# Dealing the C products of a selective scan to two engines by a fixed list, with turned pairs alternating

## The chip, the core and the metric

The kernel runs on one core of a Trainium2 chip. The core has five engines with instruction queues of their own, each worked off in order: TensorE (PE, its weight loads shown as PEld), VectorE (DVE), ScalarE (ACT), GpSimd (POOL) and SyncE (SP), which issues the transfers. The metric is the device time in microseconds (us) of one execution. The profile is one execution recorded by the hardware profiler; its span runs from the first to the last instruction of the core.

## The reference

Four images of 64 x 64 positions and 192 channels pass through four layers, called a, b, c and d in the kernel. Each layer normalizes the image, projects it, applies a short depthwise convolution and SiLU, runs a selective state-space scan along one or four orders of the positions, gates the result, projects it back and adds it to the image. The scan of one order is what matters here:

```python
xz = xs @ in_w.T ; u, z = split(xz)
uc = silu(conv(u) + cb)
dt, B, C = split(uc @ xw.T, [12, 28])        # 12 + 16 + 16 values per position
delta = softplus(dt @ dtw.T + dtb)
def step(h, inp):                            # along the positions
    dA = exp(delta[:, None] * A)             # A: channels x 16 states
    h = dA * h + (delta * u)[:, None] * B[None, :]
    y = (h * C[None, :]).sum(states)
    return h, y
```

Layers a, b and d have 384 channels in the scan, layer c has 192. Layer b scans one order of the positions, the others four. Layer a's recurrence starts anew at every row or column of 64 positions, the others run through all 4096.

## The kernel before

Everything is float32. The channels lie on the partitions, in `nb` blocks of `P`: 3 blocks of 128 for layers a, b and d, and 2 blocks of 96 for layer c. The positions are cut into chunks of `T` = 512. The 16 states of a chunk are taken in 8 pairs `j` of `NT` = 2. The unit of work is a tile: one chunk, one pair and one block, 512 positions of two states side by side, so a row of 1024 values on each partition. A chunk has 24 tiles for `nb` = 3 and 16 for `nb` = 2, in the order pair by pair, and within a pair block by block. There are 13 orders of 8 chunks in an image, 104 chunks, and 416 in the whole run: 128 each in a, c and d, 32 in b.

A tile needs these pieces of work:

- `decay`: two exponentials on ACT give dA (L534).
- `inflow` (L540): on POOL, u = du * B, where du = delta * x is the chunk's and B was spread over the partitions by a transfer. A pair whose index is in `TURNED` does it otherwise: ACT scales the transposed du by B (`scaled`, L546, 8 operations for a pair), and PE transposes the products back into PSUM (`turned_inflow`, L555, 8 transposes for a tile).
- `scan` (L564): on DVE, the recurrence h = dA * h + u; one instruction of 1024 in layer a, two of 512 in the others.
- `save_carry` (L584): the last state is kept for the next chunk; on ACT if POOL multiplies by C, else on DVE. Layer a has none.
- `outflow` (L592): the product h * C, on POOL where `pool_c` is true, else on DVE.
- `total` (L599): 8 PE transposes add the product into `py` in PSUM, and `store` (L620) copies it out by ACT and sends it off.

The buffers matter. Each tile takes one of two PSUM buffers `ps`: an ordinary tile holds dA there and reads u from SBUF, a turned tile holds u there and reads dA from SBUF. If POOL multiplies by C, the scan writes h to one of four SBUF buffers, and the PSUM buffer is free after the scan; otherwise h goes to PSUM, which is free only after the product. There are three u buffers, three for POOL's products (`cp`), two for DVE's (`c`), and four for the scaled du (`dut`).

The order on each engine is written out by hand: `keep` (L273) ties each instruction to the one before it on its engine. The loop at L661 goes over steps s, one for each tile, and issues in step s: decay of tile s+1 (of s+2 if turned), turned inflow of s+1, the scaled operations due, scan of s, ordinary inflow of s+3, POOL's product of s-1, DVE's product of s, store of s-3, and PE's totals of s-1 (DVE's product) or s-3 (POOL's). At the end of the step follows a piece of the preparation of the next chunk, by the table `at` (L472 and L479): x_proj (`p_px`), its copy and transfer (`p_dbl`), dt_proj (`p_pd`), bias (`p_pre`), `p_softplus` with its change of the activation table, `p_du` (L428), and the transposes of du.

Which engine takes a product is decided at L499 to L513 by a running count: a share of 5 in 8 goes to POOL in layer a, 2 in 3 in the others. The count runs on from chunk to chunk, so that the pattern differs between chunks, and the last pair of a chunk always goes to DVE.

Of the kernel before, what the change touches and what calls it, by code (L numbers as in the profile page):

```python
# [7 lines left out]
F32 = mybir.dt.float32  # L8
AF = mybir.ActivationFunctionType
ALU = mybir.AluOpType  # L10
# [11 lines left out]
NS = 16  # L22
DR = 12
NT = 2
TB = T // 128

TURNED = {3: (2, 4, 6, 7), 2: (1, 3, 5, 7)}
CONV_ROWS = 16
CONV_SPLIT = 37
POOL_SHORT = 5, 8  # L30
POOL_LONG = 2, 3
GN_EPS = 1e-5
LN_EPS = 1e-5

# [11 lines left out]
class Net:  # L46
# [226 lines left out]
    def keep(self, ins):  # L273

        engine = ins.ins.engine
        prev = self.pinned.get(engine)
        if prev is not None:
            self.tc.add_manual_dep(
                ins.ins, prev.name,
                mybir.DependencyInfo(mybir.DependencyClass.NoSync, mybir.DependencyReason.DATA),  # L280
                reason="program order",
            )
        self.pinned[engine] = ins.ins
        return ins

    def scans(self, sp, pp, dp, xc, P, nb, dirs, short):
# [14 lines left out]
        nc, keep = self.nc, self.keep  # L301
        zeros = None
        if short:
# [5 lines left out]
            for rev in sorted({job[2] for job in dirs}):  # L309
                fixed[rev] = []  # L310
                for k in range(3):
                    f = sp.tile([P, NT, T], F32, tag=f"dAs{rev}{k}", bufs=1, name=f"dAs{rev}{k}_a")
# [50 lines left out]
        for i in range(len(dirs)):  # L363
            for ci in range(NCH)[:: -1 if dirs[i][2] else 1]:
                c = Chunk()
# [15 lines left out]
        def channels(c, b):  # L381
            return view(xc, b, c.ci, c.o.cols) if c.xs is None else rows(c.xs[:, b, :])
# [10 lines left out]
        def spare(c, shape, name):  # L393
            return bank(max(c.n - 1, 0), nb, shape, name)

        def p_px(b):
            def f(c):
                if b == 0:
                    c.px = spare(c, [DR + 2 * NS, T], f"px_{c.key}")
                keep(nc.tensor.matmul(  # L400
                    c.px, c.o.xw[:, b, :], channels(c, b), start=b == 0, stop=b == nb - 1
                ))
            return f
# [8 lines left out]
        def p_pd(b):  # L412
            def f(c):
                c.pd = spare(c, [P, T], f"pd_{c.key}{b}")
                keep(nc.tensor.matmul(
                    c.pd, c.o.dtw[:, b * P : (b + 1) * P], c.dbl[:DR, :], start=True, stop=True
                ))
            return f

        def p_pre(b):  # L420
            def f(c):
                keep(nc.scalar.activation(c.delta[:, b, :], c.pd, AF.Identity, bias=c.o.vec[:, b, 0:1]))
            return f
# [4 lines left out]
        def p_du(c):  # L428
            c.du = sp.tile([P, nb, T], F32, tag="du", bufs=2, name=f"du_{c.key}")
            if c.xs is not None:  # L430
                x = c.xs.rearrange("p b (r w) -> p b r w", w=W)
            elif c.o.cols:
                x = xc.rearrange("p b (h w) -> p b h w", w=W)
                x = x[:, :, :, c.ci * R : (c.ci + 1) * R].rearrange("p b h w -> p b w h")
            else:
                x = xc.rearrange("p b (h w) -> p b h w", w=W)[:, :, c.ci * R : (c.ci + 1) * R, :]
            du, delta = (v.rearrange("p b (r w) -> p b r w", w=W) for v in (c.du, c.delta))
            keep(nc.gpsimd.tensor_tensor(du, delta, x, ALU.mult))

        def p_turn_B(c):  # L440
            c.tb = spare(c, [128, TB, DR + 2 * NS], f"tb_{c.key}")
# [11 lines left out]
        def p_turn_du(b):  # L453
            def f(c):
                c.td = spare(c, [128, TB, P], f"td_{c.key}{b}")
                for q in range(TB):
                    keep(nc.tensor.transpose(
                        c.td[:, q, :], c.du[:, b, q * 128 : (q + 1) * 128], self.ident[:P, :P]
                    ))
            return f  # L460
# [9 lines left out]

        if nb > 2:
            at = {  # L472
                0: [p_dir], 3: [p_px(0), p_px(1)], 4: [p_px(2)], 5: [p_dbl, p_const], 6: [p_pd(0)],
                7: [p_pre(0)], 8: [p_pd(1)], 9: [p_pre(1)], 10: [p_pd(2)], 11: [p_pre(2)],
                12: [p_softplus, p_turn_B], 13: [p_du, p_BT], 15: [p_turn_du(0)], 16: [p_duT(0)],
                17: [p_turn_du(1)], 18: [p_duT(1)], 19: [p_turn_du(2)], 20: [p_duT(2)],
            }
        else:
            at = {  # L479
                1: [p_dir], 3: [p_px(0), p_px(1)], 4: [p_dbl], 5: [p_const, p_pd(0)], 6: [p_pre(0)],  # L480
                7: [p_pd(1)], 8: [p_pre(1), p_softplus, p_turn_B], 9: [p_du, p_BT],
                10: [p_turn_du(0)], 11: [p_duT(0)], 12: [p_turn_du(1)], 13: [p_duT(1)],
            }
# [13 lines left out]
            pass  # L497

        per_chunk = NS // NT * nb  # L499
        share = POOL_SHORT if short else POOL_LONG  # L500
        tiles, due, turns = [], 0, 0
        for n, c in enumerate(chunks):
            c.n = n
            for j in range(NS // NT):
                for b in range(nb):
                    t = Tile()
                    t.c, t.b, t.j, t.n0 = c, b, j, j * NT
                    t.turned = j in TURNED[nb]
                    t.turn = turns
                    turns += t.turned  # L510
                    t.starts = b == 0
                    t.pool_c = j + 1 < NS // NT and due >= share[1]
                    due += share[0] - (share[1] if t.pool_c else 0)  # L513
                    t.key = f"{c.key}_{t.n0}{b}"
                    tiles.append(t)

# [29 lines left out]
        def scaled(c, n, q):  # L546
            if q == 0:
                c.scaled[n] = sp.tile(
                    [128, TB, nb * P], F32, tag="dut", bufs=4, name=f"dut_{c.key}_{n}"
                )  # L550
            keep(nc.scalar.activation(  # L551
                c.scaled[n][:, q, :], c.duT[:, q, :], AF.Copy, scale=c.BT[:, q, n : n + 1]
            ))
# [66 lines left out]
        def store(t):  # L620
            c, b, o = t.c, t.b, t.c.o
            if b == 0:
                c.yt = sp.tile([128, TB, nb * P], F32, tag="yt", bufs=1, name=f"yt_{c.key}")
            keep(nc.scalar.copy(c.yt[:, :, b * P : (b + 1) * P], c.py[b]))
            if b < nb - 1:
                return
            if not o.cols:
                keep(nc.sync.dma_start(
                    o.out[c.ci * T : (c.ci + 1) * T].rearrange("(q p) c -> p q c", p=128), c.yt
                ))  # L630
                return
            dst = o.out.rearrange("(h w) c -> h w c", w=W)[:, c.ci * R : (c.ci + 1) * R]
            dst = dst.rearrange("h (q k) c -> k h q c", k=128 // H)
            for k in range(128 // H):
                keep(nc.sync.dma_start(dst[k], c.yt[k * H : (k + 1) * H]))
# [10 lines left out]
        N = len(tiles)  # L646
# [11 lines left out]
                inflow(t)  # L658
        for op in scales.get(-1, []):
            scaled(*op)  # L660
        for s in range(N + 4):  # L661
            t = tiles[s] if s < N else None
            if s + 1 < N and not tiles[s + 1].turned:
                decay(tiles[s + 1])
            if s + 2 < N and tiles[s + 2].turned:
                decay(tiles[s + 2])
            if s + 1 < N and tiles[s + 1].turned:
                turned_inflow(tiles[s + 1])
            for op in scales.get(s, []):
                scaled(*op)  # L670
            if t:
                scan(t)
                if not t.pool_c and not short:
                    save_carry(t)
            if 2 <= s < N + 2 and tiles[s - 2].pool_c and not short:
                save_carry(tiles[s - 2])
            if s + 6 < N and tiles[s + 6].starts and not tiles[s + 6].turned:
                load_B(tiles[s + 6])
            if s + 3 < N and tiles[s + 3].starts:
                load_C(tiles[s + 3])  # L680
            if s + 3 < N and not tiles[s + 3].turned:
                inflow(tiles[s + 3])
            if 0 < s <= N and tiles[s - 1].pool_c:
                outflow(tiles[s - 1], nc.gpsimd)
            if t and not t.pool_c:
                outflow(t, nc.vector)
            if 3 <= s < N + 3 and tiles[s - 3].j == NS // NT - 1:
                store(tiles[s - 3])

            if 0 < s <= N and not tiles[s - 1].pool_c:  # L690
                total(tiles[s - 1])
            if 3 <= s < N + 3 and tiles[s - 3].pool_c:
                total(tiles[s - 3])
            if t and t.c.n + 1 < len(chunks):
                for f in at.get(s - t.c.n * per_chunk, []):
                    f(chunks[t.c.n + 1])
# [370 lines left out]
```

## Time and profile before

| What | us |
|---|---|
| median of 3 runs | 34516.05 (34504.28 to 34522.61) |
| profiled execution, device time | 34507.41 |
| its span | 34505.6 |
| DVE busy | 28332.2 (82%) |
| POOL busy | 25842.7 (75%) |
| PE busy | 24862.7 (72%) |
| ACT busy | 23542.8 (68%) |

The four images repeat one pattern of about 8620 us. In the first, the scans of layer a run from 302 to 2700 us of the span, those of b from 3250 to 3864, of c from 4117 to 5688, and of d from 5974 to 8437. A view of stretches gives each engine's busy time in each of these. The view of waits tells which instruction had an engine idle before it and what ended that idle time; "issue" there means that the profile shows nothing that ended it. In the timeline, equal instructions in a row are merged into one line with their count.

### The profile page before, as it was taken

The numbers are of one execution on the slowest core, as the hardware profiler recorded it, in microseconds if no ns is written. First come the engines' busy times: TensorE is split into PE (matmuls) and PEld (weight loads), VectorE is DVE, ScalarE is ACT, GpSimd is POOL, SyncE is SP. The second block draws the span as 40 slices with busy tenths as digits, with TensorE's granted clock in tenths as the row PEclk, the third lists the DMA queues.
The fourth block names the chain that finished last, engine by engine and source line by source line (L and its number), as shares of the span: only waits on it lengthen the run. The fifth ranks groups of instructions, "written<-read, shape, count | busy, mean of one in ns | idle before, by whom it ended". The sixth has DMA issues, their size and how long they took to land. (4 is left out here: it accounts for less than half of the span.)

```text
span 34505.6 us, 390569 instructions
## 1 busy us (share of the span) xinstructions
PE 24862.7 (72%) x135240; PEld 18214.6 (53%) x135240; DVE 28332.2 (82%) x23900; ACT 23542.8 (68%) x44285; POOL 25842.7 (75%) x11310
## 2 busy tenths in 40 slices
PE   7778777766777877776677787777667778777666
PEld 4554554554455455455445545545544554554554
DVE  8885798887888579888888857988878885798887
ACT  6773686776677368677667736867766773686776
POOL 5883696887688369688768836968876883696887
PEclk8888877888888877787888888778888888877888
DMA  3332333223333233322333322332233332233223
GB/s 111 107 106 79 92 106 100 93 94 115 109 105 108 78 91 106 101 93 94 115 109 106 107 79 92 107 100 93 94 115 109 105 108 78 91 106 101 93 96 111
DMA packets 1390794, 3455.73 MB, mean 100 GB/s; under 512 B 184736, under 2 KB 632080, under 8 KB 1382672
## 3 DMA queue, kind: packets, MB, share of 16 engines
q1 hardware_dynamic: 1388816, 3430.74, 31.3%
q8 instruction: 1073, 17.58, 0.2%
q14 instruction: 905, 7.41, 0.1%
HBM read 2975.18 MB, written 455.08 MB: 99 GB/s over the span
## 5 line engine op out<-in xcount | busy, mean ns | idle before, releaser
L615 PE MATMUL py_d<-ident,c_d 128*128 128x128 f32 x24576 | 3812.3, 314 | 2151.3 <-POOL c_d L597 1320.1
L615 PE MATMUL py_a<-ident,c_a 128*128 128x128 f32 x24576 | 3628.5, 302 | 2206.4 <-POOL c_a L597 1136.1
L597 POOL TENSOR_TENSOR c_d<-h_d,C_d 128x1024 f32<-128x1024 f32 x2036 | 4778.0, 2367 | 167.7 <-DVE h_d L580 164.9
L597 POOL TENSOR_TENSOR c_a<-h_a,C_a 128x1024 f32<-128x1024 f32 x1908 | 4478.4, 2370 | 422.9 <-issue 287.4
L615 PEld LDWEIGHTS py_d<-ident,c_d 128*128 128x128 f32 x24576 | 3356.9, 164 | 2603.5 <-POOL c_d L597 1640.3
L615 PEld LDWEIGHTS py_a<-ident,c_a 128*128 128x128 f32 x24576 | 3149.0, 156 | 2515.3 <-DVE c_a L597 1269.2
L542 POOL TENSOR_TENSOR u_d<-du_d,B_d 128x1024 f32<-128x1024 f32 x1536 | 3619.2, 2360 | 899.4 <-issue 885.6
L542 POOL TENSOR_TENSOR u_a<-du_a,B_a 128x1024 f32<-128x1024 f32 x1536 | 3606.6, 2363 | 715.9 <-DVE h_a L573 696.1
L597 POOL TENSOR_TENSOR c_c<-h_c,C_c 96x1024 f32<-96x1024 f32 x1356 | 3178.2, 2360 | 383.9 <-DVE h_c L580 361.1
L580 DVE TENSOR_TENSOR_SCAN h_d<-dA_d,carry_d,u_d 128x512 f32<-128x512 f32 x2536 | 3073.0, 1264 | 333.1 <-POOL c_d L597 263.6
L534 ACT ACTIVATE dA_d<-delta_d,A_d 128x512 f32<-128x512 f32 x3072 | 2118.1, 690 | 1638.0 <-DVE c_d L597 1492.5
L534 ACT ACTIVATE dA_a<-delta_a,A_a 128x512 f32<-128x512 f32 x3072 | 2119.7, 690 | 1248.8 <-DVE c_a L597 1087.6
L615 PE MATMUL py_c<-ident,c_c 96*128 96x96 f32 x16384 | 2237.3, 304 | 864.9 <-DVE c_c L597 671.9
L573 DVE TENSOR_TENSOR_SCAN h_a<-dA_a,u_a 128x1024 f32<-128x1024 f32 x1140 | 2579.5, 2281 | 328.2 <-ACT dA_a L538 175.2
L615 PEld LDWEIGHTS py_c<-ident,c_c 96*128 96x128 f32 x16384 | 2031.1, 181 | 1194.6 <-DVE c_c L597 794.4
L542 POOL TENSOR_TENSOR u_c<-du_c,B_c 96x1024 f32<-96x1024 f32 x1024 | 2411.2, 2361 | 6.3 <-DVE dA_c L580 6.0
L559 PE MATMUL ut_d<-ident,dut_d 128*128 128x128 f32 x12288 | 1913.5, 307 | 615.7 <-DVE c_d L597 589.7
L580 DVE TENSOR_TENSOR_SCAN ut_d<-dAs_d,carry_d,ut_d 128x512 f32<-128x512 f32 x1536 | 1970.8, 1283 | 395.7 <-issue 172.5
L551 ACT ACTIVATE dut_a<-duT_a,BT_a 128x384 f32<-128x384 f32 x4096 | 2291.1, 604 | 0.0
L551 ACT ACTIVATE dut_d<-duT_d,BT_d 128x384 f32<-128x384 f32 x4096 | 2290.6, 601 | 0.0
L534 ACT ACTIVATE dAs_d<-delta_d,A_d 128x512 f32<-128x512 f32 x3072 | 2042.7, 713 | 298.4 <-DVE h_d L580 230.6
L559 PEld LDWEIGHTS ut_d<-ident,dut_d 128*128 128x128 f32 x12288 | 1589.3, 159 | 1136.9 <-issue 921.3
(364 smaller groups left out, 63113.7 us busy)
## 6 DMA issues: line engine op xcount, KB each, us to landing
C_a<-bc_a SPq DMA_DIRECT2D x1024, 512.0 KB
C_d<-bc_d SPq DMA_DIRECT2D x1024, 512.0 KB
C_c<-bc_c SPq DMA_DIRECT2D x1024, 384.0 KB
B_a<-bc_a SPq DMA_DIRECT2D x512, 512.0 KB
B_d<-bc_d SPq DMA_DIRECT2D x512, 512.0 KB
B_c<-bc_c SPq DMA_DIRECT2D x512, 384.0 KB
C_b<-bc_b SPq DMA_DIRECT2D x256, 512.0 KB
xd_a<-xo_a SPq DMA_DIRECT2D x48, 2048.0 KB
```

What stands on the lines that cost most here:

```text
L534: keep(nc.scalar.activation(out, delta, AF.Exp, scale=o.A[:, t.b, k : k + 1]))
L542: keep(nc.gpsimd.tensor_tensor(t.u, t.c.du[:, t.b, None, :].to_broadcast([P, NT, T]), t.c.B[t.j], ALU.mult))
L551: keep(nc.scalar.activation(c.scaled[n][:, q, :], c.duT[:, q, :], AF.Copy, scale=c.BT[:, q, n : n + 1]))
L559: keep(nc.tensor.transpose(t.u[:, n, q * 128 : (q + 1) * 128], t.c.scaled[t.n0 + n][:, q, t.b * P : (t.b + 1) * P], self.ident,))
L573: keep(nc.vector.tensor_tensor_scan(hf, af, uf, 0.0, ALU.mult, ALU.add))
L580: keep(nc.vector.tensor_tensor_scan(hf, af, uf, o.carry[:, t.b, k : k + 1], ALU.mult, ALU.add))
L597: keep(engine.tensor_tensor(t.cm, t.h, t.c.C[t.j], ALU.mult))
L615: keep(nc.tensor.matmul(c.py[b][:, q, :], t.cm[:, n, q * 128 : (q + 1) * 128], self.ident[:P, :P], start=first, stop=c.sums[b] == NS and q ...
```

## The change

`TURNED` becomes 1, 3, 5, 7 for all layers; layers a, b and d had 2, 4, 6, 7, and layer c already had the new list. So ordinary and turned pairs alternate. The count of turned pairs stays four in eight.

The running count is replaced by a string for each number of blocks, one letter for each tile of a chunk, p for POOL and d for DVE, the same in every chunk: 17 p of 24, and 11 p of 16. The last pair is no longer kept for DVE.

In layers a, b and d the preparation is rearranged: x_proj's three matmuls stand in steps 3, 4 and 5 in place of 3, 3 and 4; the copy, the transfer of B and C, the constants of a new order and the first two blocks of dt_proj and bias come one step later; and du is computed on DVE in place of POOL, in the same step 13. Layer c keeps du on POOL and its table.

The buffers for scaled du go from four to three, and the store comes one step later, at s-4, so the loop runs one step longer.

```diff
-TURNED = {3: (2, 4, 6, 7), 2: (1, 3, 5, 7)}
+TURNED = 1, 3, 5, 7
-POOL_SHORT = 5, 8
-POOL_LONG = 2, 3
+PRODUCTS = {3: "dpdpppppdpppdpdpppdpdppp", 2: "ppdpdpppdpdpppdp"}
...
-            keep(nc.gpsimd.tensor_tensor(du, delta, x, ALU.mult))
+            keep((nc.vector if nb > 2 else nc.gpsimd).tensor_tensor(du, delta, x, ALU.mult))
...
-                0: [p_dir], 3: [p_px(0), p_px(1)], 4: [p_px(2)], 5: [p_dbl, p_const], 6: [p_pd(0)],
-                7: [p_pre(0)], 8: [p_pd(1)], 9: [p_pre(1)], 10: [p_pd(2)], 11: [p_pre(2)],
+                0: [p_dir], 3: [p_px(0)], 4: [p_px(1)], 5: [p_px(2)], 6: [p_dbl, p_const],
+                7: [p_pd(0)], 8: [p_pre(0)], 9: [p_pd(1)], 10: [p_pre(1), p_pd(2)], 11: [p_pre(2)],
                 12: [p_softplus, p_turn_B], 13: [p_du, p_BT], 15: [p_turn_du(0)], 16: [p_duT(0)],
...
-        share = POOL_SHORT if short else POOL_LONG
-        tiles, due, turns = [], 0, 0
+        tiles, turns = [], 0
...
-                    t.turned = j in TURNED[nb]
+                    t.turned = j in TURNED
...
-                    t.pool_c = j + 1 < NS // NT and due >= share[1]
-                    due += share[0] - (share[1] if t.pool_c else 0)
+                    t.pool_c = PRODUCTS[nb][len(tiles) % per_chunk] == "p"
...
-                    [128, TB, nb * P], F32, tag="dut", bufs=4, name=f"dut_{c.key}_{n}"
+                    [128, TB, nb * P], F32, tag="dut", bufs=3, name=f"dut_{c.key}_{n}"
...
-        for s in range(N + 4):
+        for s in range(N + 5):
...
-            if 3 <= s < N + 3 and tiles[s - 3].j == NS // NT - 1:
-                store(tiles[s - 3])
+            if 4 <= s < N + 4 and tiles[s - 4].j == NS // NT - 1:
+                store(tiles[s - 4])
```

## The prediction

> **What bounds the kernel now.** On the page I read the busy shares first: DVE 82%, POOL 75%, an average over stages. So I took the four scan stages of the first image apart, in the view of stretches (length, then PE, PEld, DVE, ACT and POOL busy):
>
> ```profile
> 302.00:2700.00 2398.00, 1705.79 (x10844) 1367.17 (x10844) 2076.25 (x1065) 1882.82 (x3384) 2104.30 (x893) 0.84 0.32 105
> 3250.00:3864.00 614.00, 433.53 (x2682) 363.16 (x2683) 548.50 (x514) 454.39 (x859) 528.92 (x225) 0.81 0.26 87
> 4117.00:5688.00 1571.00, 1165.24 (x6875) 926.60 (x6874) 1453.13 (x1366) 1262.82 (x2716) 1452.73 (x628) 0.71 0.34 105
> 5974.00:8437.00 2463.00, 1706.55 (x10268) 1364.95 (x10268) 2192.40 (x2051) 1854.90 (x3503) 2186.18 (x927) 0.81 0.28 92
> ```
>
> Over 32, 8, 32 and 32 chunks this is 74.9 us a chunk in a, 76.8 in b, 49.1 in c, 77.0 in d. In d DVE works 68.5 and POOL 68.3 of the 77.0: two engines nearly equal, both idle 8.5 us. Neither is the bound alone; they wait in turns. POOL's timeline in d shows where:
>
> ```profile
> 7119.29 4.67 POOL L542 TENSOR_TENSOR u_d<-du_d,B_d 128x1024 f32<-128x1024 f32 x2
> 7131.02 2.35 POOL L542 TENSOR_TENSOR u_d<-du_d,B_d 128x1024 f32<-128x1024 f32 x1 [7.06 <-issue]
> ...
> 7175.74 3.44 POOL L438 TENSOR_TENSOR du_d<-delta_d,xc_d 128x1536 f32<-128x1536 f32 x1
> 7179.13 2.36 POOL L542 TENSOR_TENSOR u_d<-du_d,B_d 128x1024 f32<-128x1024 f32 x1
> 7181.45 9.35 POOL L597 TENSOR_TENSOR c_d<-h_d,C_d 128x1024 f32<-128x1024 f32 x4
> ```
>
> The 7 us hole comes once a chunk (221 us, 32 times, in d's waits). It is the turned pairs 6 and 7 in a row: six tiles without an inflow, and the last three products held for DVE, so POOL runs dry, and its next inflow needs a u buffer that the scan of the next chunk's first tile frees. In the other 18 steps the same POOL is full (the lines after the hole run end to end), and there DVE waits for it, directly or through PE:
>
> ```profile
> DVE h_d L580 <- POOL c_d L597: 65.9, 32, 2.2
> DVE h_d L580 <- PE ut_d L559: 57.4, 33, 3.5
> DVE ut_d L580 <- issue: 45.7, 33, 2.9
> ```
>
> PE is in this list because a turned inflow stands behind totals that wait for POOL's products. In a it is the same: POOL waits 5.4 us a chunk for a u buffer (173.9 / 32) and DVE 5.7 for PE (182.6 / 32).
>
> [...]Every scan and product here has one input in PSUM; du on DVE has both in SBUF. [...]the one such instruction beside a busy POOL took 2642 ns against 559 on its own:
>
> ```profile
> L354 DVE TENSOR_TENSOR dgD_a<-ident,ds_a x4: 559/2642/2647, 272.7 to 2041.7; 128x384 f32<-128x384 f32 x4
> ```
>
> So the wait was 2.08 us, inside one POOL instruction. [...]
>
> **The change, part by part.** Durations are distances from start to start in the timelines: a POOL operation of 1024 takes 2.32 (9.35 / 4 less the overhang), a DVE tile with POOL's product 2.37 in d and 2.19 in a, one with DVE's own product and carry 3.90 in d and 3.45 in a.
>
> *Products.* Per chunk POOL's count is now 1908/128 = 14.9 in a, 15.6 in b, 10.6 in c, 15.9 in d; it becomes 17, 17, 11, 17. Over the run 504 products move: POOL +504 x 2.32 = +1169 us. DVE loses 1.26 for each in a (268) and about 1.53 elsewhere (236): -699.
>
> *du.* 288 leave POOL: 128 x 3.52 + 32 x 3.44 + 128 x 3.83 = -1051 us. No row shows it on DVE. [...]To this comes the wait for POOL's current instruction, 0 to 2.34, I take 1.0. POOL in turn stands for about 1.65. In half of d's chunks x is strided by 256 bytes, which cost POOL 4.2 in place of 3.4; on DVE 0 to 1.7 more there, I take 0.2 a chunk of d on the mean. Sum: DVE +288 x 2.7 = +780, POOL +475.
>
> So neither engine gets less work: POOL +590, DVE +80. What the change can bring is idle time alone, 8.5 us a chunk on each.
>
> *Turned pairs.* Every six tiles now have three inflows. I followed the queues by hand through one chunk. POOL's order is u6 u7 c3 u8 c4 c5 c6 c7 u12 u13 c9 u14 c10 c11 c13 u18 u19 c15 u20 c16 c17 c19 u0 u1 c21 u2 c22 c23 c1, 29 operations. In a, laid end to end from 0, c3 starts at 4.7, c9 at 23, c21 at 56, c1 at 65; DVE, held back only by u and by the four h buffers, ends those scans at least 4 us earlier each time. POOL never runs dry: 29 x 2.32 + 1.65 = **69.0** a chunk, DVE needing only 17 x 2.19 + 7 x 3.45 + 2.7 = 64.1. In d DVE needs 17 x 2.37 + 7 x 3.90 + 2.9 = **70.5**, POOL 69.0; the least slack of POOL behind a scan is about 3 us (c1). In c, POOL has 19 x 2.32 + 2.6 = **46.7**, DVE 11 x 2.36 + 5 x 3.86 = 45.3.
>
> *The preparation.* ACT must end the softplus (two table loads of 1.28 around 1.49) before du. Counting from the start of scan 12: decay 1.4, two scaled 1.1, load and softplus 2.8, so 5.3; DVE reaches du at 3.9 + 2.4 = 6.3. Then reload and decay of tile 14 end at about 8.0, while du ends at 8 to 9: du lies partly in a gap that tile 14 would leave anyway. Without that cover it costs its 2.7. PE's transposes of du, which waited 2.5 us on POOL's du (74.8 in 30 times in d), find it done. x_proj's split, and B's transfer one step later, are hidden: first use is 12 steps on. The later store and three dut buffers: the third buffer is wanted in the step after the transposes that free it; 0, at most 0.5 a chunk. SP's queue gains no transfer. *Drain:* the last three products of a stage now end on POOL: +2.5 in each of 16 stages, +40.
>
> I add idle time for in-order stalls: 1.3 in a, 1.5 in d and b, 1.3 in c. So a 70.3, d and b 72.0, c 48.0. Saving: 128 x 4.6 + 128 x 5.0 + 32 x 4.8 + 128 x 1.1 - 40 = 589 + 640 + 154 + 141 - 40 = **1484**. The profiled execution took 34507 us, 9 below the median; from the median this gives **33,030**.
>
> **Rivals.** (1) du costs its upper end on DVE (wait 2.3, stride 1.7): 160 chunks in b and d lose 1.3 more and 64 lose 1.4, 300 us in all, 33,330. For it: POOL is to be nearly full, so DVE will usually find it reading. Against: in a DVE has 5 us to spare. (2) PE's head-of-line waits stay: four turned groups still follow totals of POOL's products, and DVE keeps 5.7 in a and 3.2 in d on top of its work and my stalls: a 64.1 + 5.7 + 1.3 = 71.1, d and b 70.5 + 3.2 + 1.5 = 75, c unchanged: 128 x 3.8 + 128 x 2 + 32 x 1.8 - 40 = 760 less, 33,760. Against: these waits came from POOL being full for 18 steps and empty for 6. (3) Slower: DVE's queue stands at du. Behind du wait scan 14 and everything after it; du waits for softplus, which waits for PE's pd and pre of step 11. My margin is 1.0 us. From about 6 us of lateness per chunk (margin 1.0 plus the gain of 5) the three layers lose; at 8 us: 288 x 2 = 576 more, less 100 in c, 34,990. Against: ACT waited for pd in d at most 4.9 and on average 1.0 us. (4) No change: the stalls only move; 34,516.
>
> **Chances.** Forecast 0.70, rival 1 0.13, rival 2 0.09, rival 4 0.03, rival 3 0.05. A difference under 0.2% (70 us) can't be told from none here. Faster 0.92, same 0.03, slower 0.05. Range: the floors (69.0, 70.5, 46.7) would save 755 + 832 + 202 + 307 = 2096 and 32,420, which leaves no stall anywhere; I take 32,700 as the low end, and 33,750 as the high end, which holds rival 1 and ends at rival 2.
>
> **What would show it.** In the profile after: POOL's holes of 7 us in d and of 5.6 in a gone; POOL over 95% busy in a's scans; POOL's c rows at 2176, 544, 1408 and 2176, and none for du in a, b, d; du on DVE at 1.76 alone and up to 4.1 beside POOL; DVE's waits for PE below 2 us a chunk. The prediction is wrong if DVE waits at du for delta by microseconds, if a chunk of a still takes over 73, or if c gains more than d.

## The result, and the profile after

The changed kernel took 34610.91 us (median of 9 runs, 34565.57 to 34668.35), the kernel before beside it 34508.18 (median of 9). The ratio is 1.0029, 95% interval 1.0019 to 1.0039: slower by 0.3%, where 33,030 had been forecast. The profiled execution took 34588.73 us, its span 34586.9.

The page after, busy shares and the group of d's products on GpSimd, and the same group on the page before (busy us, mean ns, then the idle time ahead of them and what ended it):

```profile
PE 24658.1 (71%) x135240; PEld 18477.8 (53%) x135240; DVE 30202.3 (87%) x23448; ACT 23650.9 (68%) x44521; POOL 26026.2 (75%) x11526
...
L595 POOL TENSOR_TENSOR c_d<-h_d,C_d 128x1024 f32<-128x1024 f32 x2176 | 5128.5, 2376 | 1385.1 <-DVE h_d L578 1383.5
...
L597 POOL TENSOR_TENSOR c_d<-h_d,C_d 128x1024 f32<-128x1024 f32 x2036 | 4778.0, 2367 | 167.7 <-DVE h_d L580 164.9
```

DVE's busy time has grown by 30202.3 - 28332.2 = 1870 us, where the forecast added 80. The stages of the first image after, in the view of stretches (length, then PE, PEld, DVE, ACT, POOL):

```profile
302.00:2741.00 2439.00, 1714.27 (x10844) 1442.78 (x10844) 2292.14 (x1028) 1879.07 (x3374) 2153.93 (x928) 0.83 0.31 103
3292.00:3902.00 610.00, 426.90 (x2684) 366.69 (x2684) 591.40 (x500) 457.38 (x868) 533.15 (x229) 0.81 0.26 88
4158.00:5689.00 1531.00, 1121.48 (x6866) 881.16 (x6866) 1432.55 (x1340) 1266.70 (x2725) 1477.91 (x640) 0.72 0.34 107
5970.00:8479.00 2509.00, 1709.62 (x10268) 1408.47 (x10268) 2433.26 (x2011) 1868.69 (x3534) 2156.25 (x931) 0.81 0.28 90
```

A chunk takes 76.2 us in a (74.9 before), 76.3 in b (76.8), 47.8 in c (49.1) and 78.4 in d (77.0). Only c, where du stayed on GpSimd, does what was forecast (48.0); b gains 0.5. In d DVE is busy for 97% of the stage. What it is busy with shows in the lines of du, with the waits ahead of d's (shortest, median and longest, in ns):

```profile
L438 DVE TENSOR_TENSOR du_a<-delta_a,xs_a x128: 1757/10974/12598, 288.5 to 28529.6; 128x1536 f32<-128x1536 f32 x128
L438 DVE TENSOR_TENSOR du_b<-delta_b,xc_b x32: 1728/9990/10064, 3278.3 to 29690.0; 128x1536 f32<-128x1536 f32 x32
L438 DVE TENSOR_TENSOR du_d<-delta_d,xc_d x128: 1730/10562/11327, 5955.9 to 34283.1; 128x1536 f32<-128x1536 f32 x128
its engine sat idle before it (us, times) until:
...
  ACT delta_d L426: 48.1, 4
```

An instruction of 1.76 us takes 10 to 11. It does not wait for softplus: that wait occurs four times in a layer, once an image, in the first chunk. DVE's timeline around one du of d:

```profile
7110.61 2.45 DVE L578 TENSOR_TENSOR_SCAN h_d<-dA_d,carry_d,u_d 128x512 f32<-128x512 f32 x2
7112.98 10.96 DVE L438 TENSOR_TENSOR du_d<-delta_d,xc_d 128x1536 f32<-128x1536 f32 x1
7123.86 2.61 DVE L578 TENSOR_TENSOR_SCAN dA_d<-dA_d,carry_d,u_d 128x512 f32<-128x512 f32 x2
```

And POOL's at the same time:

```profile
7109.72 6.97 POOL L595 TENSOR_TENSOR c_d<-h_d,C_d 128x1024 f32<-128x1024 f32 x3
7116.66 4.66 POOL L540 TENSOR_TENSOR u_d<-du_d,B_d 128x1024 f32<-128x1024 f32 x2
7130.38 2.37 POOL L595 TENSOR_TENSOR c_d<-h_d,C_d 128x1024 f32<-128x1024 f32 x1 [9.06 <-DVE h_d L578]
```

du is issued at 7112.98, stands while POOL works off everything it has (to 7121.32), and runs then. Meanwhile the next scan stands behind du, so POOL has no h to multiply and idles for 9.06 us. The hole of 7 us that the kernel before had is gone, and one of 9 us stands in its place. Of the 1385.1 us of idle time in d's group above (167.7 before), some 935 lie in holes beside a du; the rest are shorter waits for h, and with du back on GpSimd (e1 below) most of these are gone too.

### The profile page after: what moved, and what is told of

It reads as the page before. It is cut to its first block, busy times and chain, and to the rows that moved or that the text cites. A ratio compares the mean times of both kernels' runs of the same rounds, so it can differ in the third digit from the quotient of the medians.

```text
span 34586.9 us, 388201 instructions
## 1 busy us (share of the span) xinstructions
PE 24658.1 (71%) x135240; PEld 18477.8 (53%) x135240; DVE 30202.3 (87%) x23448; ACT 23650.9 (68%) x44521; POOL 26026.2 (75%) x11526
## 5 line engine op out<-in xcount | busy, mean ns | idle before, releaser
L595 POOL TENSOR_TENSOR c_d<-h_d,C_d 128x1024 f32<-128x1024 f32 x2176 | 5128.5, 2376 | 1385.1 <-DVE h_d L578 1383.5
L595 POOL TENSOR_TENSOR c_a<-h_a,C_a 128x1024 f32<-128x1024 f32 x2176 | 5125.3, 2377 | 1083.5 <-issue 811.7
L613 PE MATMUL py_d<-ident,c_d 128*128 128x128 f32 x24576 | 3988.5, 322 | 1740.0 <-DVE c_d L595 1258.5
L613 PE MATMUL py_a<-ident,c_a 128*128 128x128 f32 x24576 | 3857.6, 313 | 1580.6 <-DVE c_a L595 847.6
L613 PEld LDWEIGHTS py_d<-ident,c_d 128*128 128x128 f32 x24576 | 3493.1, 169 | 2147.7 <-DVE c_d L595 913.4
L613 PEld LDWEIGHTS py_a<-ident,c_a 128*128 128x128 f32 x24576 | 3346.1, 163 | 1958.4 <-POOL c_a L595 940.5
L578 DVE TENSOR_TENSOR_SCAN h_d<-dAs_d,carry_d,ut_d 128x512 f32<-128x512 f32 x3072 | 3685.8, 1259 | 231.4 <-PE ut_d L557 225.1
L557 PE MATMUL ut_a<-ident,dut_a 128*128 128x128 f32 x12288 | 2004.4, 312 | 1317.2 <-DVE c_a L595 1036.8
L557 PEld LDWEIGHTS ut_a<-ident,dut_a 128*128 128x128 f32 x12288 | 1645.6, 162 | 1814.3 <-DVE c_a L595 1116.0
L578 DVE TENSOR_TENSOR_SCAN dA_d<-dA_d,carry_d,u_d 128x512 f32<-128x512 f32 x1792 | 2293.6, 1280 | 70.4 <-ACT dA_d L532 33.1
```

Of the source, the lines that this page charges most:

```text
L557: keep(nc.tensor.transpose(t.u[:, n, q * 128 : (q + 1) * 128], t.c.scaled[t.n0 + n][:, q, t.b * P : (t.b + 1) * P], self.ident,))
L578: keep(nc.vector.tensor_tensor_scan(hf, af, uf, o.carry[:, t.b, k : k + 1], ALU.mult, ALU.add))
L595: keep(engine.tensor_tensor(t.cm, t.h, t.c.C[t.j], ALU.mult))
L613: keep(nc.tensor.matmul(c.py[b][:, q, :], t.cm[:, n, q * 128 : (q + 1) * 128], self.ident[:P, :P], start=first, stop=c.sums[b] == NS and q ...
```

## The experiments

Two questions: is du the only step that failed, and why does it wait for three to five instructions of GpSimd where the trace before had shown one? SBUF and PSUM are the two on-chip memories in which the kernel keeps its tiles; each instruction's inputs lie in one or the other.

**du back on GpSimd (e1), and du alone moved in the kernel before (e2).**

```diff
 # e1, on the changed kernel; e2 is the reverse edit on the kernel before
-keep((nc.vector if nb > 2 else nc.gpsimd).tensor_tensor(du, delta, x, ALU.mult))
+keep(nc.gpsimd.tensor_tensor(du, delta, x, ALU.mult))
```

> The changed kernel with du back on GpSimd in all layers; lists, turned pairs, x_proj in three steps and all else as changed. Theory A (du on VectorE stands behind GpSimd's whole run of back-to-back instructions[...], about 7.8 us more than its 1.76 in 288 chunks, and the evening-out of GpSimd's load is a real gain): the du wait goes, GpSimd gets 288 x 3.65 = 1050 us back, chunks of a near 72, of d near 73: 33,100 to 33,500 us. Theory B (the even deal itself brings nothing, and du stood where VectorE would have stood anyway): 34,400 to 34,700.

> The kernel before with one edit: du on VectorE in layers a, b and d. Theory A: VectorE waits through GpSimd's run here too; step 13 lies in the stretch where GpSimd is full, so du takes 5 to 10 us in the median and the kernel gets slower, 35,000 to 36,000 us, although GpSimd loses 1050 us of work. Theory B: GpSimd is relieved by 3.6 us a chunk and VectorE pays 2.7: within 300 us of 34,508.

e1 took 32966.84 us, ratio to the kernel before 0.9553 (0.9539 to 0.9568), a little under the range expected. Its stretches inside a and d:

```profile
302.00:2560.00 2258.00, 1704.68 (x10748) 1429.55 (x10748) 1989.60 (x991) 1880.33 (x3370) 2239.04 (x952) 0.84 0.34 111
...
5779.00:8061.00 2282.00, 1706.97 (x10268) 1379.58 (x10268) 2131.29 (x1980) 1871.57 (x3534) 2266.47 (x962) 0.83 0.30 99
```

POOL, the last engine number, is busy for 2239.04 of 2258 us (99%): it is the bound, without holes. e2 took 36282.59 us, ratio 1.0515 (1.0499 to 1.053), more than expected. Its du took 6.5 us in a and 7.1 in d (medians), although this kernel still has its hole once a chunk:

```profile
L438 DVE TENSOR_TENSOR du_d<-delta_d,xc_d x128: 1757/7076/8045, 6178.4 to 35957.8; 128x1536 f32<-128x1536 f32 x128
```

So moving du costs 1644 us in the new order and 1774 in the old one, and everything else in the change gains 1541.

**du on DVE, with one input in PSUM (e3).** ACT copies delta into a free PSUM bank, a block at a time, and DVE makes du in three pieces:

```diff
-            keep((nc.vector if nb > 2 else nc.gpsimd).tensor_tensor(du, delta, x, ALU.mult))
+                c.dps = spare(c, [P, T], f"dps_{c.key}{b}")
+                keep(nc.scalar.copy(c.dps, c.delta[:, b, :]))
...
+                keep(nc.vector.tensor_tensor(rows(c.du[:, b, :]), rows(c.dps), channels(c, b), ALU.mult))
```

> The changed kernel with du on VectorE, but in three blocks of 512 whose delta ScalarE first copies to the spare PSUM bank (steps 13 to 15, du one step later): one input in PSUM[...]. Adds 864 copies of about 0.57 us to ScalarE. Theory A: each du takes about 0.69 us and waits for nothing, chunks of a near 70, of d near 72: 32,700 to 33,200 us, faster than with du on GpSimd. Theory C (VectorE stands there because the softplus or ScalarE's queue is late, which a duration that includes a wait would hide): no better than the changed kernel, 34,400 to 34,900.

33023.16 us, ratio 0.957 (0.9554 to 0.9586): close to e1, though not faster, as had been expected. du on DVE is then no trouble; all 384 pieces in a lie between 661 and 692 ns:

```profile
L450 DVE TENSOR_TENSOR du_a<-dps_a,xs_a x384: 661/666/692, 292.6 to 27211.4; 128x512 f32<-128x512 f32 x192
L450 DVE TENSOR_TENSOR du_d<-dps_d,xc_d x384: 660/842/1060, 5742.0 to 32722.5; 128x512 f32<-128x512 f32 x192
```

So it is not the engine that makes du slow. e3 also cuts du into three pieces and moves it one step later; that the input in PSUM alone makes the difference, the next runs show. (The second line also sizes x strided by 256 bytes: 1060 against 660 ns, so an estimate of 1.2 us for a whole du, 0.6 a chunk of d on the mean; the forecast had 0.2.)

**The wait in isolation (e4, e5).** These kernels, and e9's below, do nothing of the reference's work; their code is shown shortened. GpSimd multiplies k times in a row, and DVE comes once with two SBUF inputs (`b`) and once with PSUM in place of one (`pt`); e5 adds a late arrival, spread or common inputs, waits on ACT, and traffic of ACT, PE and transfers:

```python
for i in range(k): nc.gpsimd.tensor_tensor(o[i], g[:, :1024], b[:, :1024], ALU.mult)
nc.vector.tensor_tensor(v, b if kind == "sb" else pt, g, ALU.mult)      # 128x1536
```

> None of the reference's work is done (the output is a copy of the input): only the disputed cost by itself. GpSimd runs 1, 2, 3, 4, 6 or 8 products of 128x1024 with nothing between them; VectorE first does a product of 512 with one input in PSUM (0.7 us) and then one of 1536 with both inputs in SBUF (dvsb) or one in PSUM (dvps). Names end in a, b, c, d, f, h for 1, 2, 3, 4, 6, 8. Theory A: dvsb takes 1.7 us plus the rest of the whole run, about 1.7 + 2.32 k - 0.7, so near 10.3 for 4 and 19.6 for 8; dvps takes 1.7 to 1.8 for every k. Theory of the prediction (at most one GpSimd instruction is waited for): dvsb stays between 1.76 and 4.1 for every k.

> Again none of the reference's work (the output is a copy of the input). 8 GpSimd products of 128x1024 in a row, and one VectorE product of 1536 with both inputs in SBUF that arrives beside them; one thing differs in each trial: plain (as before), late (arrives after some 6 us), spread (every second GpSimd product reads a repeated row, as u does), small (384 values), own (VectorE reads tiles that GpSimd doesn't), chain (each GpSimd product reads a tile of ScalarE's of its own, so waits for a semaphore), act (24 ScalarE copies beside), pe (96 PE transposes beside), dma (4 spread loads of 512 KB beside), all (act, pe, dma and spread). The run alone let VectorE in after one product, the kernel doesn't. Theory D (traffic of other engines or transfers[...]): plain, small, own and late stay under 4.1 us, and one of act, pe, dma or all goes to 15 us or more. Theory E (the form of GpSimd's instructions or their waits decides): spread or chain goes long, act, pe and dma stay short. Theory F (a late arrival finds later instructions already under way): late goes long.

Timeline of DVE in e4, with `b` and k = 1, 2 and 8, then with `pt` and k = 8 (the first came when GpSimd's only product was nearly done; on its repeat it took 3.39 us):

```profile
6.37 1.75 DVE L61 TENSOR_TENSOR dvsba<-b,g 128x1536 f32<-128x1536 f32 x1
11.20 3.40 DVE L61 TENSOR_TENSOR dvsbb<-b,g 128x1536 f32<-128x1536 f32 x1
...
56.55 3.40 DVE L61 TENSOR_TENSOR dvsbh<-b,g 128x1536 f32<-128x1536 f32 x1
...
120.53 1.75 DVE L61 TENSOR_TENSOR dvpsh<-pt,g 128x1536 f32<-128x1536 f32 x1
```

The groups of e5 with 1536 values that took most and least (busy us, mean ns):

```profile
L93 DVE TENSOR_TENSOR dv_late<-b,g 128x1536 f32<-128x1536 f32 x2 | 7.6, 3780 | 0.0
...
L93 DVE TENSOR_TENSOR dv_plain<-b,g 128x1536 f32<-128x1536 f32 x2 | 4.1, 2071 | 0.2 <-ACT g L99 0.2
```

In these runs at most one instruction of GpSimd was waited for, in any company, as the prediction had it (3.40 us beside two and beside eight products, a mean of 3.78 in e5's longest group), and with an input in PSUM none (1.75 us beside eight). My explanations up to here fell. What these runs did not have was a long run of GpSimd: eight products are 18.4 us.

**The length of GpSimd's run (e9).** 40 products end to end, and DVE comes after n products of its own that read PSUM:

```python
for i in range(40): nc.gpsimd.tensor_tensor(o[i % 8], g, b, ALU.mult)     # some 93 us
for i in range(n):  nc.vector.tensor_tensor(h, pt, g, ALU.mult)           # 1.13 us each
nc.vector.tensor_tensor(dv, b, g, ALU.mult)                               # both in SBUF
```

> A measurement alone: copies of the input instead of the network, so its output is not the reference's. GpSimd runs 40 products of 128x1024 back to back (some 93 us); VectorE first does n products that read PSUM (1.2 us each), then dv, a product of 128x1536 with both inputs in SBUF, 1.76 us when nothing disturbs it. n is 4, 16, 32 and 58, so that dv comes about 5, 20, 39 and 70 us after GpSimd began; once with nothing else running (quiet), once with ScalarE, TensorE and transfers running as well (busy), and once with every second product of GpSimd taking one of VectorE's outputs (chain, full). In hole32 GpSimd is made to stand some microseconds just ahead of dv. Theory G, the length of GpSimd's run without a pause decides: dv 2.4 to 4 us at n = 4, more at 16, and from 32 on it stands through several instructions, 6 us and more, while hole32 is back at 2.4 to 4. Rival H, the length does not matter: 2.4 to 4 us in every case; then what kept VectorE out for 3 to 5 instructions in the kernel stays open.

The timeline of POOL for n = 16 and 32, and for the case with a pause (start, length, and in brackets the idle time ahead):

```profile
1521.49 93.51 POOL L73 TENSOR_TENSOR po_quiet<-g,b 128x1024 f32<-128x1024 f32 x40 [1.17 <-ACT g L111]
1616.17 92.06 POOL L73 TENSOR_TENSOR po_quiet<-g,b 128x1024 f32<-128x1024 f32 x40 [1.17 <-ACT g L111]
...
1364.44 2.34 POOL L73 TENSOR_TENSOR po_hole<-h_hole,b 128x1024 f32<-128x1024 f32 x1 [3.01 <-DVE h_hole L63]
```

And DVE's timeline for the same three, then for two cases in which every second product of GpSimd reads one of VectorE's outputs:

```profile
1539.56 2.05 DVE L109 TENSOR_TENSOR dv_quiet<-b,g 128x1536 f32<-128x1536 f32 x1
...
1652.34 57.52 DVE L109 TENSOR_TENSOR dv_quiet<-b,g 128x1536 f32<-128x1536 f32 x1
...
1365.36 3.04 DVE L109 TENSOR_TENSOR dv_hole<-b,g 128x1536 f32<-128x1536 f32 x1
...
885.06 2.75 DVE L109 TENSOR_TENSOR dv_chain<-b,g 128x1536 f32<-128x1536 f32 x1
...
1169.29 65.39 DVE L109 TENSOR_TENSOR dv_full<-b,g 128x1536 f32<-128x1536 f32 x1
```

Coming 18 us into GpSimd's run, dv takes 2.05 us. Coming 36 us into it, it takes 57.52: it ends at 1709.86, 1.63 after the last of the 40 products (1616.17 + 92.06 = 1708.23), so 24 products in a row went ahead of it. At n = 58, 66 us into the run, it is 28.14, again to the end of the run. With other engines busy the numbers are nearly the same (2.35, 58.61, 29.29). Here the turn lies at about 29 us: the last two lines are cases that came 28.8 and 29.3 us into the run (the second with other engines busy), and they took 2.75 and 65.39. Whether the time or the count of products decides can't be told, as each takes 2.3 us. A pause of 3.01 us in GpSimd just ahead of dv, and it is 3.04. In that case too VectorE had 32 products of its own behind it, as in the case of 57.52 us, so in e9 it was not its own run that counted.

The traces of the kernels fit. I followed POOL's run (gaps under 0.3 us not counted as a pause) back from every du of the changed kernel: 275 of the 288 came 30 us or more into it; 12 of these found POOL standing at that moment, and of the other 263, 240 took over 5 us, on the mean 10.7. All 240 went in only when POOL had run out of work: a hole of 7 us or more lies beside the end of each. So the three to five instructions are what POOL has left to do before it needs VectorE's next scan. In e2, 262 of the 288 took over 5 us; they mostly came some 41 us into POOL's run, and they too went in when it ended, after two or three instructions.

The other product with two SBUF inputs, dgD, came 14 us into POOL's run in the kernel before (2.64 us), 28 to 29 us after the change (1.57, 1.60 and 4.84 us in the first image), and in e1, where POOL hardly ever pauses, over 100 in 11 cases of 12 (the first of each image comes before the scans and is not counted). Its line after the change (shortest, median, longest):

```profile
L354 DVE TENSOR_TENSOR dgD_a<-ident,ds_a x16: 557/1569/4842, 271.4 to 27978.6; 128x384 f32<-128x384 f32 x16
```

And in e1:

```profile
L354 DVE TENSOR_TENSOR dgD_a<-ident,ds_a x16: 557/7768/8757, 271.0 to 26665.0; 128x384 f32<-128x384 f32 x16
```

**The same in the kernel: a pause close to du, or far from it (e13, e14).** Both add one pause a chunk to the changed kernel, in a, b and d:

```diff
+        def p_pause(c):
+            t, back = (sp.tile([128, 1], F32, tag=f"rest{i}", name=f"rest{i}_{c.key}") for i in range(2))
+            keep(nc.gpsimd.memset(t, 0.0))
+            keep(nc.gpsimd.dma_start(back, t))
+            keep(nc.gpsimd.tensor_scalar(back, back, -1.0, None, ALU.mult))
...
 # e13
-                7: [p_pd(0)], 8: [p_pre(0)], 9: [p_pd(1)], 10: [p_pre(1), p_pd(2)], 11: [p_pre(2)],
+                7: [p_pd(0)], 8: [p_pre(0), p_pause], 9: [p_pd(1)], 10: [p_pre(1), p_pd(2)], 11: [p_pre(2)],
 # e14
-                17: [p_turn_du(1)], 18: [p_duT(1)], 19: [p_turn_du(2)], 20: [p_duT(2)],
+                17: [p_turn_du(1)], 18: [p_duT(1)], 19: [p_turn_du(2)], 20: [p_duT(2), p_pause],
```

> The changed kernel, du on VectorE, with a pause in GpSimd's order in step 8 of each chunk of a, b and d, five steps ahead of du: GpSimd sends one value per partition from SBUF to SBUF by a transfer and its next instruction waits for it[...]. If the length of GpSimd's run without a pause keeps VectorE out (14 us: one instruction; 28 us: two; 33 us and more: until GpSimd runs dry), du comes some 5 to 15 us after the pause and takes 2 to 4 us in place of 9 to 11; the pause costs GpSimd up to 3 us a chunk, du's wait falls by 6, so the time falls below the changed kernel's 34,611, to 33,400 to 34,000. If the length is not the cause, du stays at 9 to 11 and the pause is added: 34,900 to 35,500.

> The same kernel with the same pause in step 20, some 17 steps (50 us) ahead of the next du, so that GpSimd's run has grown long again when du comes. If the length of the run decides: du 9 to 11 us as without the pause, and the time between 34,600 (the pause hidden) and 35,500 (3 us more in each of 288 chunks). If any pause or the transfer itself helps: as with the pause shortly ahead of du.

e13 took 33565.31 us, ratio 0.9727 (0.9711 to 0.9743), e14 34574.39, ratio 1.002 (1.0013 to 1.0028). The pause in POOL's timeline of e13:

```profile
7055.88 0.14 POOL L442 MEMSET rest_d<- 128x1 f32 x1
7056.31 0.59 POOL L443 DMA_DIRECT2D rest_d<-rest_d  x1 [0.29 <-POOL rest_d L442]
7059.68 0.21 POOL L444 TENSOR_SCALAR rest_d<-rest_d 128x1 f32<-128x1 f32 x1 [2.77 <-DMA rest_d<-rest_d]
```

The lines of du in e13 (shortest, median, longest):

```profile
L438 DVE TENSOR_TENSOR du_a<-delta_a,xs_a x128: 1757/2834/14409, 292.9 to 27704.1; 128x1536 f32<-128x1536 f32 x128
L438 DVE TENSOR_TENSOR du_d<-delta_d,xc_d x128: 1758/3391/12796, 5841.9 to 33262.0; 128x1536 f32<-128x1536 f32 x128
```

And in e14:

```profile
L438 DVE TENSOR_TENSOR du_a<-delta_a,xs_a x128: 1757/9273/10984, 292.0 to 28579.3; 128x1536 f32<-128x1536 f32 x128
L438 DVE TENSOR_TENSOR du_d<-delta_d,xc_d x128: 1731/10764/12789, 5953.8 to 34269.5; 128x1536 f32<-128x1536 f32 x128
```

The same three instructions keep POOL from its products for some 4 us a chunk in e13 and 2.4 in e14. Placed close ahead of du they make the kernel 1046 us faster than the changed one; placed far from it they leave it where it was (37 us less, a little under the least that was expected). In e14, where du comes mostly 45 us or more after the pause, 142 of 288 stand for 10.5 us on the mean; the other 146 take 1.76 and were not held at all, and most of these came when POOL had run dry or was just doing so, which brings the kernel nothing; why POOL runs dry there was not followed. In e13 du comes within 16 us of the pause, and 281 of 288 take under 5 us, on the mean 2.7. So in the kernel too, as far as these two runs show it, the length of GpSimd's run is what holds du up.

It is not a hard rule, and the kernels have no fixed turn: 7 du of e13 still stood, for 11 us on the mean, 8 to 12 us into the run, and dgD in e14, 24.6 us into it, stood for 6.2 to 6.4 us in 8 cases of 12 and took 1.5 in the other 4. Nor does an old run always hold to its end. In e13 dgD came some 59 us into the run; after three instructions it went in without any pause, beside a short instruction of POOL (128x48), in all 12 cases. DVE first, then POOL:

```profile
840.02 6.18 DVE L354 TENSOR_TENSOR dgD_a<-ident,ds_a 128x384 f32<-128x384 f32 x1
...
841.10 4.66 POOL L601 TENSOR_TENSOR c_a<-h_a,C_a 128x1024 f32<-128x1024 f32 x2
845.73 0.68 POOL L346 TENSOR_SCALAR A_a<-A_a 128x48 f32<-128x48 f32 x1
846.38 4.68 POOL L601 TENSOR_TENSOR c_a<-h_a,C_a 128x1024 f32<-128x1024 f32 x2
```

**The other parts of the change (e6, e10, e11).** The turned pairs alone, the product list alone (with the later store), and both without the new x_proj steps; du is on GpSimd in all three:

```diff
 # e6, on the kernel before
-TURNED = {3: (2, 4, 6, 7), 2: (1, 3, 5, 7)}
+TURNED = {3: (1, 3, 5, 7), 2: (1, 3, 5, 7)}
 # e10, on the kernel before; e11 has TURNED = 1, 3, 5, 7 and three dut buffers as well
-                    t.pool_c = j + 1 < NS // NT and due >= share[1]
+                    t.pool_c = PRODUCTS[nb][len(tiles) % per_chunk] == "p"
```

> The kernel before with one edit: turned pairs 1, 3, 5, 7 in all layers; the running count, the last pair on VectorE, x_proj and du on GpSimd stay. Theory A (the gain comes from filling GpSimd's hole, most of which is two turned pairs in a row): 33,300 to 33,800, some two thirds of what the changed kernel with du on GpSimd gains. Rival (the fixed list is what counts, since GpSimd's share and the last pair make the hole): 34,200 or more.

> The kernel before with the fixed list of products (and the later store that it needs), but the turned pairs 2, 4, 6, 7, the old x_proj table, and du on GpSimd. GpSimd has 29 operations and du in a chunk, 70.8 us, VectorE under 68, so if the list alone opens the gain (the last pair's products no longer wait for VectorE), the time is near that with du back on GpSimd, 32,970 to 33,300. If list and alternating pairs are needed together (the turned pairs 6 and 7 leave GpSimd without inflows for six tiles), 33,700 to 34,600. I lean to the middle of the two, 33,600.

> The changed kernel with du back on GpSimd, and x_proj and what follows it in the steps they had before. Theory: this part costs and brings nothing, so 32,967 as with the new table, within 100. Rival: the new steps take matmuls of x_proj off the point where TensorE holds up a scan, worth 0.3 us in a chunk or more: 33,060 or above with the old table.

e6: 34671.18 us, ratio 1.0047 (1.0032 to 1.0062), so the gain expected of it did not come. POOL's hole is still there, likely because the last pair's products still go to DVE (no run changes these alone):

```profile
7161.30 4.68 POOL L597 TENSOR_TENSOR c_d<-h_d,C_d 128x1024 f32<-128x1024 f32 x2 [7.15 <-DVE h_d L580]
```

e10: 33746.25, ratio 0.9779 (0.9764 to 0.9793). e11: 33077.35, ratio 0.9587 (0.9571 to 0.9603). So the list brings some 760 us alone, alternating pairs (with three `dut` buffers) some 670 on top of it, while without it they lose 163, and the x_proj steps some 110 more (e11 less e1; the two intervals just don't overlap, 0.9568 and 0.9571). In the first image's a, POOL's du waits for delta 28 times in e11 (15.9 us) and 5 times in e1 (3.0 us): the preparation comes later with the old steps. It was not followed further.

**Better versions (e7, e8, e12).** All start from e1. With POOL as the bound, e7 gives it one product less in a (16 of 24), e12 in b and d too; e8 uses e3's PSUM du in a alone:

```diff
-PRODUCTS = {3: "dpdpppppdpppdpdpppdpdppp", 2: "ppdpdpppdpdpppdp"}
+PRODUCTS = {3: "dpdpdpppdpppdpdpppdpdppp", 2: "ppdpdpppdpdpppdp"}    # e12; in e7 for layer a alone
```

> The changed kernel with du on GpSimd and one more product of layer a's chunks on VectorE (tile 4: 16 of 24 on GpSimd there). If GpSimd is the bound in a once du is back on it (29 x 2.32 + 3.5 = 70.8 us a chunk, measured 70.6), each chunk of a loses up to 2.3 us: 32,670 to 32,850. If VectorE's waits for PE hold it instead: 32,950 or more.

> du on GpSimd in layers b, c and d; in layer a on VectorE in three blocks with delta from PSUM; all else as changed. From the two runs of which it is made, layer a saves 18 us an image on one and b and d some 43 us on the other: 32,850 to 32,950, faster than either by 0.1 to 0.4%.

> The changed kernel with du back on GpSimd and 16 products of 24 on GpSimd in all three layers with three blocks, where the list with 16 in layer a alone took 32,675. In b and d GpSimd comes down from 71.3 to 69.0 us a chunk, VectorE goes up from about 67.6 to 69.1. If GpSimd is the bound there, 160 chunks gain up to 1.8 us: 32,400 to 32,600. If the two engines hold each other up once they are even: 32,650 to 32,900.

e7 took 32674.69 us, ratio 0.9469 (0.9453 to 0.9484), e8 32840.13, ratio 0.9516 (0.9502 to 0.953; 10 us under its range), e12 32762.53, ratio 0.9491 (0.9477 to 0.9505). e7 is the best, 5.3% under the kernel before: a comes to 68.9 us a chunk (from 71.0). In b and d, going from 17 to 16 brings nothing more (d's stage 2293 us against 2284, by PE's first and last total); by the count of e12's expectation the two engines are even there.

## Why the prediction was wrong, step by step

- **du, the wait. This is the step that failed**: "the wait for POOL's current instruction, 0 to 2.34, I take 1.0". Over all 288, du took 240 x 10.67 + 48 x 2.11 = 2662 us on DVE, not the 780 of the sum; less 1.76 each the mean wait is 7.5. Of the 2.7 a du in that sum, what the wait of 1.0 leaves was the author's estimate of du's own length, and it came close: with nothing to wait for du took 1.73 to 1.76 (the shortest of each layer, above), and the trace before has a sum of the same size on DVE, with both inputs in SBUF, at 1.72 to 1.76 (`y_d`, L720 and L722, 64 times). The upper end was no bound, so rival 1 (33,330) was too kind as well. The evidence was one row, dgD at 2.64 in the kernel before, and it was read rightly for that place: POOL had paused 14 us earlier. du's place is another. In the prediction's own lines POOL comes out of its hole at 7131.02 and reaches du at 7175.74, 44.7 us later with no pause over 0.3 us between, and e2 shows that du on DVE stood there in the old order too (6.5 to 7.1 us). So the price was carried from a young run of GpSimd to an old one. In the changed order POOL also had four or five instructions left at that place, where in e2 it had two or three. A wait of at most one GpSimd instruction is what was measured where GpSimd's run was young (dgD 2.64 us at 14 us, e9's dv 2.05 at 18); 36 us into the run e9's dv took 57.52, to the end of the run.
- **du, POOL's side.** "POOL 475" was to be its standing behind du, about 1.65 us each; in e9, GpSimd's 40 products took 93.51 us with dv inside the run and 92.06 with dv at its end, so an estimate of 1.45 for a dv of the same size. It became a hole of 7 to 9 us in most chunks (9.06 above), as the scans queue behind du on DVE. POOL is busy for 88% of a's scans (2153.93 of 2439 us), where over 95% was to show the forecast right.
- **du's place.** Right: softplus was in time, and rival 3's reason did not occur. Its consequence did, DVE's queue standing at du, with another cause; at 5.7 us a chunk (1644 / 288) it came out near that rival's break-even of 6.
- **Products and turned pairs.** Right as a whole: with du on GpSimd (e1) the chunks are 71.0, 70.4, 48.3 and 71.3 in a to d, against the forecast's 70.3, 72.0, 48.0, 72.0, and the time is 63 us from 33,030. That it is so near is in part luck: e1 swaps one cost for another, as POOL has du's 3.5 again, in place of standing for 1.65. The working priced the two edits together and could not say that the pairs alone bring nothing.
- **The preparation, "hidden".** Wrong by some 110 us: the new x_proj steps gain a little.
- **PE's waits "below 2 us a chunk".** Right in d (52.2 us in 31 chunks), not in a (114.9, so 3.7).
- **What was to show it wrong** was right: "DVE waits at du for delta" did not happen, but a chunk of a took over 73, and c gained (1.3 us) while d lost. Rival 2 (PE's waits, 75 us in d) is excluded by e1's 71.3. The drain of 40 us and the three `dut` buffers were not measured apart.

## What to carry to other kernels

Before an instruction with two SBUF inputs is put on VectorE, look at how long GpSimd has been running without a pause at the place where it will stand: here a wait measured shortly after a pause (2.05 us, 18 us into e9's run; 2.64 for dgD) said nothing about one long after it (57.52 us, 36 us into the run), even in the same kernel (10.67 us on the mean for 240 du). If GpSimd is full there, bring one of the inputs into PSUM (e3, 33023.16 us), leave the instruction on GpSimd (e1, 32966.84), or give GpSimd a pause close ahead of it (e13, 33565.31; 34610.91 without). Where GpSimd was the bound and full, moving one product in 24 off it (e7, 292 us under e1) was worth more than moving a's du with an input in PSUM (e8, 127 under e1); it needs room on VectorE in that stage.

## What the runs showed of the hardware

- An instruction of VectorE with two SBUF inputs got in after at most one GpSimd instruction of 128x1024 where GpSimd's run was young (e9, 18 us: 2.05 us), and only at the run's end where it was old (e9, 36 us: 57.52 us, 24 products; in the changed kernel all 240 du that took over 5 us, 10.67 on the mean). The turn was near 29 us in e9 (2.75 us at 28.8, 65.39 at 29.3); in the kernels it was not fixed (24.6 us in e14, where dgD took 6.2 to 6.4 or 1.5, and 8 to 12 us for 7 du of e13, 11 us on the mean), and in e13 dgD, 59 us into the run, went in beside a short GpSimd instruction of 128x48 (6.18 us). In e9 a pause of 1.17 us between the cases was enough: 18 us into the next run dv took 2.05 us. Why an old run kept VectorE out stays open; no run here looks inside GpSimd.
- With one input in PSUM the instruction was not held up: 1.75 us beside eight products in e4, as the shortest with both in SBUF, and 661 to 692 ns for all 384 pieces of du in e3's layer a.
- A transfer of one value per partition, issued by GpSimd and waited for by it, held GpSimd for about 4 us in e13 (7055.88 to 7059.89), and for some 2.4 in e14 (25003.76 to 25006.16 for one of them).
